# Turning an involution unit's sums with VectorE blocks and DRAM transfers instead of TensorE

## The chip, the cores and the metric

The kernel runs on one core of one Trainium2 chip. The metric is device time in microseconds for one execution, and the number compared is the median of several. Five engines work in parallel: TensorE (PE in the profile; its weight loads are PEld), VectorE (DVE), ScalarE (ACT), GpSimd (POOL) and SyncE (SP), which here issues nearly all transfers. Each has its own instruction stream; semaphores order them. SBUF and PSUM tiles have 128 partitions[...].

## The reference

Four images of 512 channels, 64 x 64 pixels, all float32. The first layer is self-attention over the 4096 pixels of an image, the second an involution: a 7 x 7 filter whose weights differ from pixel to pixel and are shared by 16 channels.

```python
# layer 0
q, k, v = wq@x + bq, wk@x + bk, wv@x + bv          # 128 channels each
attn = softmax(einsum('bci,bcj->bij', q, k))       # 4096 x 4096
x = wo @ einsum('bcj,bij->bci', v, attn) + bo + x
# layer 1
o1 = relu((W1 @ x) * s1 + b1)                      # 128 channels
w  = Ws @ relu((Wr @ o1) * sr + br) + bs           # 49 taps x 8 groups per pixel
inv[c, h, w_] = sum over 49 taps of w[group(c), tap, h, w_] * o1[c, h+dy, w_+dx]
x = (W3 @ inv) * s3 + b3 + x
```

## The kernel before, in words

An image is worked through in eight chunks of 512 pixels (eight rows). `keys_values` computes keys and values of all chunks at the start of an image. `attention` then takes one chunk of queries at a time: 32 steps, each with a score matmul (`pss`), an exponential on ACT (`pt`), a matmul with the values (`po`) and an addition on DVE of `pt` into the running denominators (`pacc`, L646). One step takes about 1.7 us on TensorE. There are five `pt` buffers, two PSUM buffers for scores and two PSUM buffers of the tag "mm", which all the small matmuls share.

Everything else is woven into these steps. After each step `chores` advances three generators by a step: `finishing` (denominators, output projection `pwo`, its addition to `x` on DVE, the first layer of the involution `o1`), `closing` (below), and `involution`. How far each may advance is decided while the program is written out, by a running estimate `pe` of TensorE's time and the estimates `free` of the other engines. A scheduling layer then settles the order of each engine's stream from its own expectations; the engines carry that order out as it stands.

The `involution` works in units of four image rows: 16 units per image, two to a chunk. The pixels of a unit lie on partitions, so a unit's sums `acc` have shape 128 pixels x (2 x 4 x 128). DVE multiplies shifted pixel rows by weights (`prod`, L341), POOL adds the product to `acc` (L365), and two last POOL additions fold the four partial rows together (L376). The pixel rows come through DRAM: `finish_block` turns `o1` in blocks of 32 x 32 on DVE (`o1t`, L559), writes them to the DRAM image `pix` (L569), and `pump` reads windows of `pix` into an SBUF ring of twelve rows (L247).

`turn_unit` is the part that is changed. The last layer W3 needs the channels on partitions, so the sums of a unit must be turned from pixels x channels to channels x pixels. Before, TensorE transposes two 128 x 128 tiles per unit into a "mm" PSUM buffer `pa` (L393), ACT copies them to `accT` (L404), and after the second unit of a chunk `close_chunk` is queued: four matmuls `py` with W3, one "mm" buffer each, four DVE additions `x<-py` into the chunk `x` (L419), each of which frees its buffer, and the transfer of the finished chunk to `out` (L428). The chunk's buffer, one of six, is then loaded with a later chunk (L173).

In the fourth image, units that end after attention is done add on TensorE and turn their sums there together; these are not touched, and neither are any units of the fourth image.

Of the kernel before, what the change touches and what calls it, by code (L numbers as in the profile page):

```python
# [8 lines left out]
F32 = mybir.dt.float32  # L9
# [4 lines left out]
B, C, H, W = 4, 512, 64, 64  # L14
N = H * W
P = 128
CT = C // P
CH = 512
# [33 lines left out]
NT = UR // 2  # L52
# [15 lines left out]
DVE_OP, POOL_OP = 0.7, 1.28  # L68
# [6 lines left out]
TB = 32  # L75
# [6 lines left out]
def fast_path(  # L82
# [20 lines left out]
    nc = tc.nc  # L103

    def pool(name, bufs, **kw):
        return ctx.enter_context(tc.tile_pool(name=name, bufs=bufs, **kw))
# [6 lines left out]
    work1 = pool("work1", 1)  # L113
    work2 = pool("work2", 2)
    prods = pool("prods", 4)
    scratch = pool("scratch", 1, space=bass.MemoryType.DRAM)
# [18 lines left out]
    ring = const.tile([P, RING, K, P], F32, name="ring")  # L135
    pix = [
        scratch.tile([H + 2 * PAD, WP, P], F32, tag=f"pix{i}", name=f"pix{i}") for i in range(2)
    ]

    x_r = x.rearrange("b (t p) n -> b p t n", p=P)  # L140
# [6 lines left out]
    finishing, closing, units = [], [], []  # L147
# [4 lines left out]
    reds, sums_c = {}, {}  # L152
# [5 lines left out]
    def until(us):  # L158
        while pe < us and not tail:
            yield "wait"  # L160

    def pe_us(us):
        nonlocal pe
        pe += us

    def takes(engine, us):
        free[engine] = max(free[engine], pe) + us
        return free[engine]
# [33 lines left out]
    def w_slice(off, t):  # L202
        return wt[:, off + t * P : off + (t + 1) * P]

    def v1(i):
        return vec[:, i : i + 1]

    def mm(o, lhsT, rhs, start=True, stop=True, shared=1):
        pe_us(rhs.free_size() * PE_COLUMN / shared)
        return nc.tensor.matmul(o, lhsT=lhsT, rhs=rhs, start=start, stop=stop)  # L210
# [80 lines left out]
    def involution():  # L291
        nonlocal low, due
        while True:
# [80 lines left out]
            if accp is None:  # L374
                for n in (2, 1):
                    nc.gpsimd.tensor_tensor(  # L376
                        acc[:, :, :n, :], acc[:, :, :n, :], acc[:, :, n : 2 * n, :], ALU.add
                    )
            closing.append(turn_unit(b, u, acc, accp, takes("pool", POOL_OP * 1.5)))


    def turn_unit(b, u, acc, accp, done):
        c, k = divmod(u, 2)
        yield from until(done + 2.0)
        for _ in range(7 if tail else 0):
            yield
        last = (b, c) == (B - 1, NCH - 1)
        if last or k == 0:
            sums_c[b, c] = work1.tile([P, CH], F32, tag="accT", name=f"accT_{b}_{c}")
        pa = ps.tile([P, NT, P], F32, tag="mm", name=f"pa_{b}_{u}")  # L390
        if accp is None:
            for t in range(NT):
                nc.tensor.transpose(pa[:, t, :], acc[:, t, 0, :], ident)  # L393
            pe_us(0.25)
        else:

            accs = work1.tile([P, CH // P, P], F32, tag="o1t", name=f"accs_{b}_{u}")
            nc.scalar.copy(accs, accp.rearrange("p t d c -> p (t d) c"))
            for t in range(NT):
                parts = [acc[:, t, d, :] for d in range(4)] + [accs[:, 2 * t + d, :] for d in range(2)]  # L400
                for i, part in enumerate(parts):
                    mm(pa[:, t, :], part, ident, i == 0, i == len(parts) - 1)
        n = NT * P
        nc.scalar.copy(sums_c[b, c][:, k * n : (k + 1) * n], pa.rearrange("p t c -> p (t c)"))  # L404
        yield
        if last:
            closing.append(close_chunk(b, c, k * n, n, sums_c.pop((b, c))))
        elif k:
            closing.append(close_chunk(b, c, 0, CH, sums_c.pop((b, c))))


    def close_chunk(b, c, off, n, acc):
        xt = xs[b, c][:, :, off : off + n]
        yield
        for t in range(CT):
            py = ps.tile([P, CH], F32, tag="mm", name=f"py_{b}_{c}_{off}_{t}")[:, :n]
            mm(py, w_slice(O_W3, t), acc[:, off : off + n])
            takes("dve", DVE_OP * n / CH)
            nc.vector.scalar_tensor_tensor(  # L419
                xt[:, t, :], py, v1(V_S3 + t), xt[:, t, :], ALU.mult, ALU.add  # L420
            )
            if n < CH:
                nc.sync.dma_start(out_r[b, :, t, c * CH + off : c * CH + off + n], xt[:, t, :])
            for _ in range(2):
                yield
        takes("dma", X_US)
        if n == CH:
            nc.sync.dma_start(out_r[b, :, :, c * CH + off : c * CH + off + n], xt)  # L428
# [553 lines left out]
def attention_then_involution(tc, x, wts, vecs, out):  # L982
    nc = tc.nc
    with tc.tile_pool(name="verdict", bufs=1) as vpool:
        verdict = vpool.tile([1, 1], mybir.dt.int32, name="verdict")
        fast_path(tc, x, wts, vecs, out, verdict)
        again = nc.values_load(verdict[0:1, 0:1], min_val=0, max_val=1)
        with tc.If(again > 0):
            general_path(tc, x, wts, vecs, out)
# [85 lines left out]
```

## Time and profile before

| | |
|---|---|
| median of 3 runs | 2623.66 us (2622.92 to 2625.16) |
| the profiled execution | 2624.13 us, of which the span of the trace is 2622.3 us |
| TensorE busy | 2599.3 us, 99% |
| DVE busy | 1865.5 us, 71% |
| POOL busy | 1821.0 us, 69% |
| ACT busy | 857.2 us, 33% |
| transfers, mean busy share of the 16 DMA engines | 36% |
| span less TensorE's busy time | 23.0 us |

Busy time counts an engine's own work and not its waiting. A wait of another engine only matters where TensorE ends up waiting for it. Line numbers are those of the kernel before.

### The profile page before, as it was taken

Reading aid. Unit: us, or ns where it says so; the run is one execution under the profiler, and the core shown is the slowest. Engines: PE = TensorE matmul, PEld = TensorE weight load, DVE = VectorE, ACT = ScalarE, POOL = GpSimd, SP = SyncE. Lnnn points to the kernel's source line nnn. Section 1 sums busy time; section 2 is a strip of 40 time slices with the busy share of each in tenths; the row PEclk is TensorE's granted clock in tenths of the full one; section 3 lists DMA queues with packets and bytes.
Section 4 is the critical chain, followed back from the end, with each engine's and each line's share of the span. In section 5 each row is a group of like instructions: output and inputs, shape, how many; then the busy total and the mean of one; then the engine's idle time right before and its main releaser. Section 6 shows DMA issues by size and latency. Waiting matters only on the chain.

```text
span 2622.3 us, 24098 instructions
## 1 busy us (share of the span) xinstructions
PE 2599.3 (99%) x7382; PEld 1242.0 (47%) x7382; DVE 1865.5 (71%) x2626; ACT 857.2 (33%) x1430; POOL 1821.0 (69%) x1197
## 2 busy tenths in 40 slices
PE   9999999999999999999999999999999999999998
PEld 7444444445544444444554444444464444444574
DVE  0347887877575787888576677878757768787887
ACT  1333333332233333333223333333313333333330
POOL 0007887878781787888875467888787667777876
PEclk9999999999999999999999999999999999999999
DMA  6032323336514244322541433434453423222343
GB/s 235 0 74 60 75 64 75 69 89 156 139 40 106 60 93 92 87 71 61 153 116 36 103 61 92 93 92 93 92 154 88 107 60 89 68 61 60 77 91 101
DMA packets 143898, 231.70 MB, mean 88 GB/s; under 512 B 57032, under 2 KB 63632, under 8 KB 143632
## 3 DMA queue, kind: packets, MB, share of 16 engines
q1 hardware_dynamic: 143328, 229.71, 36.2%
q8 instruction: 60, 0.98, 0.2%
q14 instruction: 78, 0.64, 0.1%
q10 hardware_dynamic: 432, 0.36, 0.0%
HBM read 187.28 MB, written 42.77 MB: 88 GB/s over the span
## 4 chain that ended last, share of the span: by engine, by line
PE 94%; POOL 3%; DVE 2%; DMA 0%; issue 0%; ACT 0%; POOLq 0%; DVEq 0%; ACTq 0%
PE pss L210 34%; PE po L210 33%; PE pq L210 4%; PE pwo L210 4%; PE p L210 4%; PE py L210 4%; PE pv L210 4%; PE pk L210 3%; POOL acc L365 3%; PE pw L210 2%; DVE prod L341 1%; PE pr L210 1%; PE pa L393 0%; PE accp L210 0%; DVE x L419 0%
## 5 line engine op out<-in xcount | busy, mean ns | idle before, releaser
L365 POOL TENSOR_TENSOR acc<-acc,prod 128x768 f32<-128x768 f32 (+3 forms) x1063 | 1699.0, 1616 | 777.0 <-DVE prod L341 726.2
L210 PE MATMUL pss<-q,k 128*128 128x512 f32 (+1 forms) x2112 | 1055.0, 584 | 2.3 <-ACT q L471 2.3
L210 PE MATMUL po<-pt,v 128*128 128x512 f32 (+1 forms) x2112 | 1047.5, 580 | 0.0
L615 ACT ACTIVATE pt<-pss 128x512 f32<-128x512 f32 x1024 | 611.5, 597 | 1225.6 <-PE pss L210 1201.7
L341 DVE TENSOR_TENSOR prod<-ring,pw 128x512 f32<-128x512 f32 (+3 forms) x1092 | 902.1, 850 | 100.7 <-POOL acc L365 87.7
L646 DVE TENSOR_TENSOR pacc<-pacc,pt 128x512 f32<-128x512 f32 x958 | 666.2, 695 | 379.7 <-ACT pt L615 372.9
L210 PEld LDWEIGHTS po<-pt,v 128*128 128x128 f32 x2112 | 399.3, 190 | 480.3 <-issue 460.2
L210 PEld LDWEIGHTS pss<-q,k 128*128 128x128 f32 x2112 | 389.6, 190 | 452.3 <-issue 432.6
L210 PE MATMUL py<-accT,wt 128*128 128x512 f32 (+1 forms) x264 | 132.8, 586 | 7.8 <-DVE x L419 6.7
L210 PE MATMUL pwo<-on,wt 128*128 128x512 f32 (+1 forms) x264 | 129.3, 583 | 0.0
L210 PEld LDWEIGHTS pv<-wt,x 128*128 128x128 f32 x1024 | 121.7, 195 | 15.8 <-issue 15.6
L515 DVE SCALAR_TENSOR_TENSOR x<-pwo,bo,x 128x512 f32<-128x512 f32 (+1 forms) x132 | 96.3, 734 | 45.5 <-PE pwo L210 44.0
L376 POOL TENSOR_TENSOR acc<-acc 128x512 f32<-128x512 f32 x120 | 119.5, 996 | 9.4
L210 PE MATMUL pv<-wt,x 128*128 128x128 f32 x1024 | 123.3, 279 | 0.0
L341 DVE TENSOR_TENSOR acc<-ring,pw 128x1024 f32<-128x1024 f32 (+1 forms) x84 | 79.4, 964 | 61.1 <-PE pw L210 58.9
L533 ACT ACTIVATE x<-x,vec 128x512 f32<-128x512 f32 (+1 forms) x132 | 92.8, 706 | 81.5 <-PE p L210 76.4
L210 PE MATMUL p<-x,wt 128*128 128x512 f32 (+1 forms) x264 | 119.2, 579 | 0.0
L210 PE MATMUL pk<-x,wt 128*128 128x512 f32 x256 | 117.1, 597 | 0.3 <-DMA x<-x_dram 0.3
L419 DVE SCALAR_TENSOR_TENSOR x<-py,vec,x 128x512 f32<-128x512 f32 (+1 forms) x132 | 95.9, 726 | 29.8 <-PE py L210 28.1
L210 PE MATMUL pq<-x,wt 128*128 128x512 f32 (+1 forms) x264 | 115.5, 580 | 0.0
L210 PEld LDWEIGHTS py<-accT,wt 128*128 128x128 f32 x264 | 49.3, 191 | 65.3 <-issue 48.5
L210 PEld LDWEIGHTS pq<-x,wt 128*128 128x128 f32 x264 | 49.8, 190 | 58.7 <-issue 56.4
(58 smaller groups left out, 723.0 us busy)
## 6 DMA issues: line engine op xcount, KB each, us to landing
x<-x_dram SPq DMA_DIRECT2D x55, 1024.0 KB, 6.0
ring<-pix SPq DMA_DIRECT2D x74, 448.0 KB, 10.9
ring<-pix SPq DMA_DIRECT2D x24, 1344.0 KB, 18.3
out_dram<-x SPq DMA_DIRECT2D x31, 1024.0 KB, 4.4
ring<-pix SPq DMA_DIRECT2D x24, 896.0 KB, 14.0
ring<-pix SPq DMA_DIRECT2D x30, 672.0 KB, 11.2
ring<-pix SPq DMA_DIRECT2D x6, 2240.0 KB, 19.1
pix<-o1t SPq DMA_DIRECT2D x192, 32.0 KB, 1.7
```

The costliest lines, as they stand in the source:

```text
L210: return nc.tensor.matmul(o, lhsT=lhsT, rhs=rhs, start=start, stop=stop)
L341: nc.vector.tensor_tensor(prod[:, :, p0 : p0 + n, :].rearrange("p t d (g c) -> p t d g c", g=G), image.rearrange("p t d (g c) -> p t d g c ...
L365: nc.gpsimd.tensor_tensor(acc[:, :, d0 : d0 + n, :], acc[:, :, d0 : d0 + n, :], prod[:, :, :n, :], ALU.add,)
L376: nc.gpsimd.tensor_tensor(acc[:, :, :n, :], acc[:, :, :n, :], acc[:, :, n : 2 * n, :], ALU.add)
L419: nc.vector.scalar_tensor_tensor(xt[:, t, :], py, v1(V_S3 + t), xt[:, t, :], ALU.mult, ALU.add)
L515: nc.vector.scalar_tensor_tensor(xt[:, t, :], pw, bo[:, t : t + 1], xt[:, t, :], ALU.add, ALU.add)
L533: nc.scalar.activation(xt[:, t, :], xt[:, t, :], AF.Identity, bias=v1(V_B3 + t))
L615: nc.scalar.activation(pt, pss, AF.Exp)
L646: nc.vector.tensor_tensor(paccs[k], paccs[k], pt, ALU.add)
```

## The change

In `turn_unit`, for every unit of the first three images, the two TensorE transposes and the ACT copy are replaced. DVE turns the sums in blocks of 32 x 32 within each strip of 32 partitions into a tile `turned` (two buffers). SP writes its four strips of 32 partitions to a DRAM scratch tile `turns` (two buffers, alternating by chunk), placed so that the blocks land at their final channels and pixels. After the second unit of a chunk SP reads the chunk's `turns` back as `accT` with channels on partitions. Pauses of three steps of the closing queue stand between the turn and the writes, between the writes and the read, and between the read and `close_chunk`. The tile `accT` is now made when it is read back and not at the first unit.

```diff
+    turns = [
+        scratch.tile([CH // P, P, P], F32, tag=f"turns{i}", name=f"turns{i}") for i in range(2)
+    ]
...
         yield from until(done + 2.0)
         for _ in range(7 if tail else 0):
             yield
+        if accp is None and b < B - 1:
+            blocks = work2.tile([P, NT * P], F32, tag="turned", name=f"turned_{b}_{u}")
+            takes("dve", DVE_OP * NT * P / CH)
+            nc.vector.transpose(
+                blocks.rearrange("p (t k q) -> p t k q", t=NT, q=TB),
+                acc[:, :, 0, :].rearrange("p t (k q) -> p t k q", q=TB),
+            )
+            for _ in range(3):
+                yield
+            turn = turns[c % 2]
+            for i in range(P // TB):
+                rows = slice(i * TB, (i + 1) * TB)
+                nc.sync.dma_start(
+                    turn[k * NT : (k + 1) * NT, :, rows]
+                    .rearrange("t (k a) q -> a (t k) q", a=TB),
+                    blocks[rows].rearrange("p (k q) -> p k q", q=TB),
+                )
+            if k:
+                for _ in range(3):
+                    yield
+                sums_c[b, c] = work1.tile([P, CH], F32, tag="accT", name=f"accT_{b}_{c}")
+                nc.sync.dma_start(
+                    sums_c[b, c].rearrange("p (t x) -> p t x", x=P),
+                    turn.rearrange("t c x -> c t x"),
+                )
+                for _ in range(3):
+                    yield
+                closing.append(close_chunk(b, c, 0, CH, sums_c.pop((b, c))))
+            return
         last = (b, c) == (B - 1, NCH - 1)
```

## The prediction

> **What bounds the kernel now.** I read the chain of waits first. It lies on TensorE almost throughout:
>
> ```profile
> PE 94%; POOL 3%; DVE 2%; DMA 0%; issue 0%; ACT 0%; POOLq 0%; DVEq 0%; ACTq 0%
> ```
>
> So each microsecond of matmul taken away is a microsecond won, as long as nothing makes TensorE wait. Next, the transposes by their tile and one of them in TensorE's timeline:
>
> ```profile
> L393 PE MATMUL pa<-ident,acc x120: 272/273/329, 240.6 to 2536.7; 128*128 128x128 f32 x120
> ...
> 320.54 1.02 PE L210 MATMUL po<-pt,v 128*128 128x512 f32 x2
> 321.39 0.38 PE L393 MATMUL pa<-ident,acc 128*128 128x128 f32 x2
> 321.61 1.02 PE L210 MATMUL pss<-q,k 128*128 128x512 f32 x2
> ```
>
> The 273 ns are a pipelined duration. What a pair costs is seen from start to start: 321.61 - 321.39 = 0.22 us. Last, TensorE's waits: it hardly waits, and what it does wait for is DVE freeing a PSUM buffer of `py`, the three times where an image begins:
>
> ```profile
> PE py L210 <- DVE x L419: 6.7, 3, 2.4
> ```
>
> **What the skill says.** The Trainium skill, "PSUM — Partial Sum Buffer", section "Engine vs sequencer instructions": the queues of ScalarE, VectorE and GpSimd are strict FIFO. An operation that waits holds all behind it. The trace of before agrees: at 1327.06 us a `prod` waits 2.67 us for the ring and everything behind stands. "VectorE: DVE Perf Modes", "The three transpose paths": VectorE turns 32 x 32 blocks only, so the crossing between strips is left to the transfers; the trace shows the same pair for `o1t`. "DMA: Bandwidth & Descriptors", "Anatomy of one DMA — SWDGE (gpsimd) path": about 2.0 us fixed per DMA. The kernel's like transfers, issued by SP, land in 1.7 us.
>
> **The change part by part.**
>
> *Removed.* 48 units x one pair x 0.22 us = **10.4 us** of TensorE, all on its path. 48 ACT copies of 0.37 us go too and win nothing: ACT is busy 33%.
>
> *Added on DVE.* 48 block turns of 128 x 256. The nearest row is the turn of 128 x 512 at L559, 707 ns; half is 0.36 us (bounds 0.3 and 0.7). 17 us in all on an engine 71% busy, beside TensorE: nothing by itself.
>
> *Added on SP.* 192 writes of 32 KB, like this row, and 24 reads of 256 KB, which I put at 2.5 to 4.1 us from the 128 KB and 256 KB rows:
>
> ```profile
> pix<-o1t SPq DMA_DIRECT2D x192, 32.0 KB, 1.7
> ```
>
> After the last turn of a chunk that is some 4 x 0.5 + 1.7 + 4 = 8 us. In the built program's order `py` stands 30 us and more behind the second turn (neighbouring steps at 344 and 379 us for chunk 1), with SP quiet in between. I cost the detour itself at nothing; its cover is those steps. Chunk by chunk `py` moves about 20 us back (chunk 1: 360 to 379 us), so the chunk's output and the next load go back too. Chunk 6 has its buffer at about 330 us instead of 311 and is used at 460: nothing. The odd case is the start of an image, below.
>
> *Moved: what DVE now waits for.* This is the part that decides. Before, the transposes waited for POOL's final sum inside TensorE's stream, in most units 6 to 9 us after it was there. In the built program the turn stands in DVE's stream much earlier, among steps that ran before POOL was done. For each of the 48 units I compared the end of the DVE operation just ahead of the turn with the end of POOL's last addition, both in the trace of before: POOL is later every time, by 2.2 to 8.8 us, 5.6 on average. So DVE will stand still some 270 us in all. It has the room, and the `pacc` behind the turn do too: `pt` has five buffers, and TensorE would only miss a `pacc` that is about 9 us late. What has no such room is `x<-py`, which frees one of two "mm" buffers. Unit 4 of image 0, in the built order:
>
> ```
> DVE:  turned_0_4, pacc, x<-py_0_1_0_0, pacc, pacc, x<-py_0_1_0_1
> PE:   py_0_1_0_0, pss, po, pss, po, pr, py_0_1_0_1, pw, pw, ...
> ```
>
> `py_1` takes the buffer of `py_0` (`pr` has the other). POOL's and TensorE's timelines around it:
>
> ```profile
> 375.06 7.69 POOL L365 TENSOR_TENSOR acc<-acc,prod 128x512 f32<-128x512 f32 x8
> 382.83 2.08 POOL L376 TENSOR_TENSOR acc<-acc 128x512 f32<-128x512 f32 x2
> ...
> 382.43 1.02 PE L210 MATMUL po<-pt,v 128*128 128x512 f32 x2
> 383.38 0.65 PE L210 MATMUL pr<-o,wt 128*64 128x256 f32 x4
> 383.96 0.93 PE L210 MATMUL pw<-wt,red 33*128 33x392 f32 x4
> ```
>
> The sums are there at 384.91. Then DVE: turn 0.36, `pacc` 0.70, `x<-py` 0.73; the buffer is free at 386.7. TensorE came to this place at 383.96, and now has three `py` (0.86 us each) and a transpose pair less behind it: 383.96 - 2.58 - 0.22 = 381.2. POOL does not come earlier, it ran without a gap from 354.7 us on. **Idle: 5.5 us.** Unit 10 has the same order with one more `pacc`: POOL ends at 601.22, free at 603.7; TensorE arrives at 600.30 + 0.86 (`pw` is now ahead) - 2.80 = 598.4: 5.3 us. In unit 2 `x<-py` follows the turn at once: 312.3 + 0.36 + 0.73 = 313.4 against 311.7: 1.7 us. Per image 12.5 us; the same places recur in images 1 and 2 with the same distances.
>
> *The start of an image.* `turned_12` stands ahead of `o1t_7` on DVE, and its writes ahead of the writes of `o1t_7` on SP. Image 1:
>
> ```profile
> 1300.77 0.70 DVE L559 STREAM_TRANSPOSE o1t<-o 128x512 f32<-128x512 f32 x1
> ...
> 1327.06 0.42 DVE L341 TENSOR_TENSOR prod<-ring,pw 128x256 f32<-128x256 f32 x1 [2.67 <-DMA ring<-pix]
> ```
>
> POOL ends unit 12 at 1309.6, so `o1t_7`, and behind it `pix` and the ring, go back by about 9 us, for a `prod` that already waits on the ring. A 1 MB output that went ahead of the ring is now behind it and gives back 2 to 4 us. Seven late products later comes the new image's first `pacc`, which has some 5 us of room: 1 to 4 us of TensorE idle, I take 2.5. The 2.2 us that TensorE lost there on `py` before (6.7 in 3) should go, since those `py` stand later: 0.3 net per image.
>
> *Sum.* 3 x (12.5 + 0.3) - 10.4 = +28 us on the profiled execution's 2624.1, and the median of the runs lies 0.5 us under that: **2652 us**, 1.1% slower. A measurement of this kernel can tell about 0.2% (5 us) from no change.
>
> **Rivals.**
>
> *TensorE does not wait and the 10.4 us are won.* For it: transfers have 30 us of cover, DVE has idle time, POOL is in no hurry. The mechanism is POOL's lead: at units 2, 4 and 10 it would have to end 2 to 6 us earlier against TensorE than in the trace of before, and from 1.2 us of idle per place (10.4 / 9) on, the change loses. Against it: POOL ran unit 4 without a gap. Time 2613, or 2607 if the waits at the image starts go too.
>
> *The waits only cancel.* If TensorE's lead of 2.8 us is used up otherwise, the idle is 2.7, 2.5 and 0 per image, 15.6 in all, and without the image starts the result is +5: 2629.
>
> *Worse: the units fall behind.* The wait at a turn puts the next unit back by up to 4 us. POOL took 32.7 us for unit 4, from its first product at 352.2, and a unit has 36. If the delay is carried on, every unit's turn catches `pacc` and `x<-pwo` as well, and each of 24 chunks loses 2 us more: 2700.
>
> *Transfers late.* If reads land 20 us late behind ring loads (18 us for the largest), some `py` wait for DMA. Cover of 30 us speaks against it; 3 image starts x 5 us would be +15 on the forecast, 2667.
>
> *It does not do what it says:* the built order shows the pairs gone and the turns there; excluded.
>
> **How the numbers follow.** Won without waits 0.15; cancel 0.13; waits at the nine places 0.52, 2635 to 2672 by itself; transfers late 0.10; falling behind 0.10. The range runs from 2612, the win, to 2685, which leaves out most of falling behind. Slower by over 0.2%: 0.74; within 0.2%: 0.08, the middle of cancelling; faster: 0.18.
>
> **What would show it.** TensorE's busy time down by about 10 us and its idle up by about 40; a wait "PE py <- DVE x" of some 35 us in nine or more times, the longest near 5; DVE waiting some 270 us for POOL at the turn; no wait of `py` for `accT`. Right about the work and wrong about the wait if "PE py <- DVE x" stays under 10 us; wrong about the transfers if `py` waits for DMA.

## The result, and the profile after

The changed kernel takes **2661.1 us** (median of 4 runs, 2659.99 to 2663.23) against 2624.41 us of the kernel before on the same chip: ratio 1.0141, 95% interval 1.0128 to 1.0153. It is slower by 36.7 us; the prediction said 28 us, 2652, and its range held the time. The profiled execution took 2659.99 us, of which the span is 2658.2 us, so the spans differ by 35.9 us. One execution in the experiments, of the kernel with transfers only, ran in a slower state of the chip (2728.14 us, granted clock 0.948) and is left out of its ratio. Line numbers from here on are those of the changed kernel, or of the experiment named.

The chain of waits is no longer nearly all TensorE. POOL, DVE, transfers and a share with nothing to wait for ("issue") have grown in it:

```profile
PE 81%; POOL 8%; issue 4%; DVE 4%; DMA 2%; SPq 1%; ACT 0%; POOLq 0%; DVEq 0%; ACTq 0%
```

The list of TensorE's waits (what waits, for what; us in total, times, longest) answers the single line of before, 6.7 us in three waits:

```profile
PE py L215 <- DVE x L454: 18.6, 10, 2.8
PE pss L215 <- ACT pt L650: 13.0, 4, 4.3
PE p L215 <- DVE x L550: 3.1, 1, 3.1
```

The first line is the predicted wait, at half the predicted size. The second is the late start of the images, predicted smaller; the third was not foreseen. DVE's list shows where the lateness starts, and that it is not DVE's work: the turn itself is one short row of the page, with its idle time in the last column.

```profile
DVE turned L396 <- POOL acc L381: 238.2, 48, 8.7
DVE pacc L681 <- ACT pt L650: 237.3, 216, 4.9
...
DVE prod L346 <- DMA ring<-pix: 44.4, 10, 8.6
```

```profile
L396 DVE STREAM_TRANSPOSE turned<-acc 128x256 f32<-128x256 f32 x48 | 21.4, 446 | 238.2 <-POOL acc L381 238.2
```

The transfers of the detour, in the list of DMA issues (KB each, median us to landing), are as quick as the like ones of before:

```profile
turns<-turned SPq DMA_DIRECT2D x192, 32.0 KB, 1.7
accT<-turns SPq DMA_DIRECT2D x24, 256.0 KB, 2.8
```

Unit 4 of image 0 again, the place that the prediction worked through: POOL, DVE and TensorE in the timeline of the changed kernel.

```profile
381.47 2.06 POOL L381 TENSOR_TENSOR acc<-acc 128x512 f32<-128x512 f32 x2
...
383.57 0.45 DVE L396 STREAM_TRANSPOSE turned<-acc 128x256 f32<-128x256 f32 x1 [4.42 <-POOL acc L381]
383.94 0.67 DVE L681 TENSOR_TENSOR pacc<-pacc,pt 128x512 f32<-128x512 f32 x1
384.51 0.73 DVE L454 SCALAR_TENSOR_TENSOR x<-py,vec,x 128x512 f32<-128x512 f32 x1
...
380.06 1.02 PE L215 MATMUL pss<-q,k 128*128 128x512 f32 x2
...
381.87 0.65 PE L215 MATMUL pr<-o,wt 128*64 128x256 f32 x4
385.30 1.12 PE L215 MATMUL py<-accT,wt 128*128 128x512 f32 x2 [2.77 <-DVE x L454]
386.35 1.54 PE L215 MATMUL pw<-wt,red 33*128 33x392 f32 x4
387.82 2.07 PE L215 MATMUL pss<-q,k 128*128 128x512 f32 x2
389.69 1.92 PE L215 MATMUL po<-pt,v 128*128 128x512 f32 x2
```

Read down the middle: the turn waits for POOL, then `pacc`, then `x<-py`, which ends at 385.24, and TensorE's next `py` starts at 385.30. That is the predicted chain, step for step. What was not predicted stands in the last two lines: a pair of score matmuls takes 2.07 us there, and 1.02 us at 380.06. The windows view gives the granted clock of such stretches (start:end, length, TensorE's busy time and instructions, clock, DMA share, GB/s):

```profile
375.00:395.00 20.00, 17.23 (x38) 0.83 0.53 101
...
300.00:320.00 20.00, 17.65 (x46) 1.00 0.40 76
1350.00:1370.00 20.00, 16.13 (x32) 0.83 0.62 141
```

In the trace's clock records TensorE's clock drops to 0.500 for 3.4 or 6.8 us around many of its pauses. This costs time that no wait shows, and lengthens TensorE's *busy* time.

I therefore split each span in three: the gaps between TensorE's matmuls, half of the time at clock 0.500 outside these gaps, and the rest.

| kernel (span, us) | gaps | lost at half clock | rest |
|---|---|---|---|
| before (2622.3) | 16.2 | 5.1 | 2601.0 |
| changed (2658.2) | 43.8 | 19.5 | 2594.9 |
| turn held in place (2604.5) | 9.7 | 1.7 | 2593.1 |
| turn only (2646.0) | 31.8 | 10.4 | 2603.8 |
| transfers only (2623.5) | 15.9 | 6.8 | 2600.8 |
| removal only (2610.3) | 14.0 | 5.1 | 2591.2 |
| held in unit 12 (2643.5) | 30.6 | 18.1 | 2594.8 |
| held in units 2, 4, 10 (2628.1) | 24.1 | 9.9 | 2594.1 |
| `py` later (2618.0) | 16.0 | 8.5 | 2593.5 |

The last column is steady: 2601 to 2604 where TensorE's transposes are there, 2591 to 2595 where they are gone. So the 35.9 us are + 27.6 of gaps, + 14.4 of half clock and - 6.1 of the rest. The removal alone should have brought some 10 in that column; about 4 us are not accounted for.

### The profile page after: what moved, and what is told of

It reads as the page before. It is cut to its first block, busy times and chain, and to the rows that moved or that the text cites. A ratio compares the mean times of both kernels' runs of the same rounds, so it can differ in the third digit from the quotient of the medians.

```text
span 2658.2 us, 24165 instructions
## 1 busy us (share of the span) xinstructions
PE 2607.4 (98%) x7286; PEld 1232.9 (46%) x7286; DVE 1870.4 (70%) x2674; ACT 838.0 (32%) x1382; POOL 1822.4 (69%) x1197
## 4 chain that ended last, share of the span: by engine, by line
PE 81%; POOL 8%; issue 4%; DVE 4%; DMA 2%; SPq 1%; ACT 0%; POOLq 0%; DVEq 0%; ACTq 0%
PE pss L215 28%; PE po L215 28%; POOL acc L370 7%; PE pq L215 4%; PE pv L215 4%; PE py L215 3%; PE pwo L215 3%; PE pk L215 3%; PE p L215 3%; PE pw L215 2%; DVE prod L346 2%; DMA ring<-pix 2%; POOL acc L381 1%; DVE pacc L681 1%; DVE x L454 1%
## 5 line engine op out<-in xcount | busy, mean ns | idle before, releaser
L396 DVE STREAM_TRANSPOSE turned<-acc 128x256 f32<-128x256 f32 x48 | 21.4, 446 | 238.2 <-POOL acc L381 238.2
L215 PE MATMUL py<-accT,wt 128*128 128x512 f32 (+1 forms) x264 | 134.9, 594 | 19.4 <-DVE x L454 18.6
## 6 DMA issues: line engine op xcount, KB each, us to landing
ring<-pix SPq DMA_DIRECT2D x6, 2240.0 KB, 19.5
```

What stands on the lines that cost most here:

```text
L396: nc.vector.transpose(blocks.rearrange("p (t k q) -> p t k q", t=NT, q=TB), acc[:, :, 0, :].rearrange("p t (k q) -> p t k q", q=TB),)
```

## The experiments

My theory (W): the removal wins about 10 us; the turn stands in DVE's stream ahead of the time at which POOL is done, DVE waits there, and whatever stands close behind the turn and is needed by TensorE comes late. The rivals: the transfers cost the time, through the queue or through late data; or DVE's standing time as such does.

### The turn held in its place in the source

`keep_in_program_order` tells the scheduling layer to leave an instruction behind what the source puts ahead of it.

```diff
-            nc.vector.transpose(
+            tc.keep_in_program_order(nc.vector.transpose(
                 blocks.rearrange("p (t k q) -> p t k q", t=NT, q=TB),
                 acc[:, :, 0, :].rearrange("p t (k q) -> p t k q", q=TB),
-            )
+            ))
```

> The changed kernel with one thing different: the DVE turn keeps its place in the order in which the program is written, behind the DVE operations written before it, 5 to 14 us later in DVE's stream than in the changed kernel and after POOL's last sum. Transfers, steps and removed transposes are those of the changed kernel. Theory W (the loss comes from DVE standing at the turn and waiting for POOL, with x<-py and the late products behind it): the wait of DVE at the turn falls from 238 us to under 15 us, the waits of TensorE for x<-py and for pt at the image starts go, and so do the stretches of half clock that follow them; time 2606 to 2617 us, faster than before. Theory T (the detour through DRAM costs it: 216 more transfers on SP's queue and their small packets): the transfers are all still there, so 2650 us or more.

Measured: 2607.49 us (2606.3 to 2607.93, 5 runs), ratio to before 0.9937, interval 0.9924 to 0.9951. The wait at the turn is gone from DVE's list, and no wait in TensorE's list, apart from the program's start and the last image, is longer than 0.8 us:

```profile
PE pss L215 <- ACT q L506: 2.3, 3, 0.8
...
PE pq L215 <- DVE x L454: 0.8, 1, 0.8
```

The same turns and the same transfers, with another place for the turn, make a kernel that is 54 us faster than the changed one and faster than the kernel before. So neither the turn's work nor the detour is the price; the place is.

### One part at a time: turn, transfers, removal

The first puts the turn into the kernel before and uses its result for nothing; the transposes stay.

```diff
+        if accp is None and b < B - 1:
+            blocks = work2.tile([P, NT * P], F32, tag="turned", name=f"turned_{b}_{u}")
+            takes("dve", DVE_OP * NT * P / CH)
+            nc.vector.transpose(
+                blocks.rearrange("p (t k q) -> p t k q", t=NT, q=TB),
+                acc[:, :, 0, :].rearrange("p t (k q) -> p t k q", q=TB),
+            )
```

> The kernel before, with TensorE's transposes and ACT's copies kept, and one DVE turn of each unit's sums added, whose result nothing reads; no transfers. In the built order the turn stands as early as in the changed kernel, but x<-py, which has not been moved, stands ahead of it in units 2, 4 and 10. It tells the wait at the turn from what stands behind it. Theory W: DVE waits 200 to 270 us for POOL, TensorE's waits for x<-py stay near 7 us, and only the image starts lose (o1t of the last chunk behind the turn of unit 12, then the ring, then the first pacc): 3 x (4 to 8) us, so 2634 to 2648 us. Theory T: no transfer was added, so 2624 plus or minus 4 us.

Measured: 2649.22 us (2647.83 to 2652.07, 4 runs), ratio 1.0100, interval 1.0084 to 1.0115. DVE's and TensorE's waits, in this order:

```profile
DVE turned L390 <- POOL acc L376: 234.2, 48, 8.7
```

```profile
PE py L210 <- DVE x L426: 16.8, 3, 5.7
PE p L210 <- DVE x L522: 2.6, 1, 2.6
```

DVE stands as long as in the changed kernel, but TensorE pays mainly at three places, the image starts, with 5.5 to 5.7 us each, where it lost 2.1 to 2.4 us before. The expectation missed here: these waits are for `x<-py`, and the first `pacc` of an image costs nothing; the time lies 1 us above its range. At units 2, 4 and 10 nothing happens: with the transposes in place, `py` runs where it ran before, away from the next turn. So those waits need two parts of the change together, the early turn and the detour that puts `py` some 20 us back, close behind a turn.

The second adds the 192 writes and 24 reads to the kernel before, from a weight tile and into a tile that nobody uses.

```diff
+            turn = turns[c % 2]
+            for i in range(P // TB):
+                rows = slice(i * TB, (i + 1) * TB)
+                nc.sync.dma_start(
+                    turn[k * NT : (k + 1) * NT, :, rows]
+                    .rearrange("t (k a) q -> a (t k) q", a=TB),
+                    wt[rows, : NT * P].rearrange("p (k q) -> p k q", q=TB),
+                )
+            if k:
+                spare = work1.tile([P, CH], F32, tag="spare", name=f"spare_{b}_{c}")
+                nc.sync.dma_start(
+                    spare.rearrange("p (t x) -> p t x", x=P), turn.rearrange("t c x -> c t x")
+                )
```

> The kernel before, complete, and beside it the 192 writes and 24 reads of the changed kernel, with the same shapes and the same scratch tiles, taking their data from a weight tile that is ready from the start, into a tile that nothing reads; no DVE turn. Theory W: transfers are covered, 2624 plus or minus 5 us. Theory T: 216 issues and 13 MB in 128-byte and 512-byte pieces delay the ring and the loads, 2640 to 2665 us.

Measured: 2624.96 us (2622.83 to 2625.59, 12 runs), ratio 1.0002, interval 0.9993 to 1.0010. TensorE's list begins with the line of before:

```profile
PE py L213 <- DVE x L436: 6.7, 3, 2.4
```

The transfers cost nothing that can be measured.

The third takes the transposes and copies out of the first three images and puts nothing in their place; `py` multiplies a weight tile instead of the sums.

```diff
+        if accp is None and b < B - 1:
+            yield
+            if k:
+                closing.append(close_chunk(b, c, 0, CH, wt[:, :CH]))
+            return
```

> The kernel before, leaving out the transposes of the sums and the copies in the first three images; py multiplies a weight tile instead of the sums, so the involution's share of the output of these images is left out. It measures the term of 10.4 us by itself. Expected 2624 - 10.4 = 2613 to 2614 us if 0.22 us per pair is right, down to 2607 us if the waits for x<-py at the image starts go with it. If the pairs were hidden by something, 2620 us or more.

Measured: 2612.16 us (2610.31 to 2613.34, 5 runs), ratio 0.9954, interval 0.9941 to 0.9968: 11.5 us won (8 to 15 by the interval), 0.24 us for a pair if all of it is theirs. In the table the last column falls by 9.8 us, 0.20 us for a pair, and the gaps by 2.2. The old `py` waits at the image starts stay, 6.9 us in three.

### Where the turn hurts

Two runs hold the turn in place for some units only.

```diff
+            if u == 12:
+                tc.keep_in_program_order(turned)
```

> The changed kernel with the turn held at the place of the source text (behind what the source puts ahead of it in VectorE's stream) for unit 12 alone, the last unit of an image. It isolates the start of the next image. Theory W (each turn that stands early makes VectorE wait for POOL, and what is queued behind that turn comes late to TensorE: here the sums that free turned_12's followers up to the first pacc): TensorE's waits of its pss on ACT's pt at the image starts (4 of them, 13.0 us, in the changed kernel) go, with the part of TensorE's slow clock that follows those pauses (some 5 us); its py waits for x (10, 18.6 us) stay. About 2643 us, 2639 to 2647, against 2661.1. Rival R (the image start is late because the transfers of the turned sums, 48 writes and 24 reads, stand in front of the pixel ring's loads in the queues): the pss waits stay at about 13 us and the time at 2658 to 2663.

Measured: 2645.41 us (2643.37 to 2649.01, 5 runs), ratio 1.0081, interval 1.0067 to 1.0094. TensorE's list:

```profile
PE py L215 <- DVE x L456: 18.0, 9, 2.8
PE p L215 <- DVE x L552: 2.8, 1, 2.8
...
PE pss L215 <- ACT pt L652: 0.8, 3, 0.3
```

The `pss` waits are gone but for 0.8 us and the `py` waits stay, as W said. By itself this does not rule out the rival, because the writes of unit 12 have moved together with its turn: they are issued from 688.98 us on, behind the first loads of the ring, where the changed kernel had them ahead. The traces together do. At the first image start the ring's loads begin at 674.00 us before, at 684.81 with the turn only and no transfer of turned sums, and at 686.47 in the changed kernel. So of the 12.5 us by which the ring is later the turn alone brings 10.8, which leaves 1.7 for the transfers in front of it and all else. This one turn per image is worth some 16 us (1.0141 - 1.0081 = 0.60% of 2625; the two intervals leave about 5 us either way). I had put 18: the half clock fell by only 1.4 us and not by 5.

```diff
+            if u in (2, 4, 10):
+                tc.keep_in_program_order(turned)
```

> The changed kernel with the turn held at the place of the source text for units 2, 4 and 10 alone. Theory W: TensorE's py waits for x (10, 18.6 us) go, with the part of the slow clock that follows them (some 12 us of the 14); the pss waits at the image starts (4, 13.0 us) stay. About 2631 us, 2626 to 2637. Rival Q (any turn that stands early costs in like measure, since VectorE's lateness only moves to the next unit): the py waits reappear at units 3, 5 and 11 or at others, sum 12 us or more, and the time is 2648 or above.

Measured: 2630.38 us (2629.85 to 2632.6, 11 runs), ratio 1.0023, interval 1.0014 to 1.0032. TensorE's list begins:

```profile
PE pss L215 <- ACT pt L652: 11.8, 3, 4.2
PE p L215 <- DVE x L552: 3.1, 1, 3.1
```

No `py` wait for `x` is left, and none has moved to other units. Three turns per image are worth 31 us, of which the gaps are 43.8 - 24.1 = 19.7 and the half clock 9.6. The two runs together make up 47 of the 54 us; what remains holds, among others, the `p` wait of 3.1 us, which both keep.

### The turn left early, `py` moved away from it

A longer pause in the closing queue keeps every turn early, but puts 17 to 27 DVE operations between the turns of units 2, 4 and 10 and the next `x<-py`, where the changed kernel has none to two.

```diff
-                for _ in range(3):
+                for _ in range(8):
                     yield
                 closing.append(close_chunk(b, c, 0, CH, sums_c.pop((b, c))))
```

> The changed kernel with the sums of a unit's last chunk closed later in the source (8 steps of the stream in place of 3 between the attention product and its closing), which leaves every turn early in VectorE's stream but puts 20 or more VectorE operations between a turn and the next copy x<-py behind it. Theory W: VectorE still waits some 240 us at the turn, but the copy is no longer late: the py waits of units 2, 4 and 10 (18.6 us) go; the pss waits at the image starts (13 us) stay or grow, since x comes later there. 2628 to 2640. Rival V (the sheer time that VectorE stands at the turn, 238 us, costs TensorE, wherever the copy is): the time stays within 5 us of 2661 with other waits of the same sum.

Measured: 2617.68 us (2615.26 to 2620.2, 8 runs), ratio 0.9971, interval 0.9961 to 0.9982. DVE's list first, the first line of TensorE's second:

```profile
DVE turned L396 <- POOL acc L381: 228.0, 48, 8.7
DVE pacc L681 <- ACT pt L650: 222.0, 201, 4.9
```

```profile
PE pk L215 <- DMA x<-x_dram: 6.7, 3, 2.3
```

DVE stands 228 us at the turn, nearly as long as in the changed kernel, and the kernel is faster than before. So nearly all of the standing time costs nothing, and rival V falls: `pacc`, behind the turn, waits less for `pt` in turn. Before, that wait was

```profile
DVE pacc L646 <- ACT pt L615: 372.9, 342, 4.9
```

and here it is 222.0 us. What the standing time may still cost is at most the 9 us (0.9971 - 0.9937 of 2624) by which this run is slower than the turn held in its place.

My expectation was wrong in one half, and the time lies 10 us below its range. I had the `pss` waits at the image starts stay; they went too, and TensorE waits there for `x` to be loaded, 2.2 to 2.3 us before each. SP's timeline at the first of them shows what holds up the load:

```profile
666.32 1.81 SPq L405 DMA_DIRECT2D turns<-turned  x4
...
670.19 0.40 SPq L178 DMA_DIRECT2D x<-x_dram  x1
```

It stands in SP's queue behind the writes of unit 12's turn and four writes of `o1t`, and that turn ended only at 666.29, after 8.75 us of waiting for POOL. Issued at 670.19, the load lands 5.9 us later, and `pk` starts at 676.20. The order is the same at the other two image starts. So these 6.7 us, too, hang on the late turn, by way of the transfer queue. That the pause at `pk` gives the ring the time that `pss` lacked is possible, but no run separates it.

Of all versions, the turn held in its place is the fastest: 2607.5 us, with the detour through DRAM kept.

## Why the prediction came out as it did

*Removal.* 10.4 us predicted, 11.5 measured on its own, with 8 to 15 as its interval. Right.

*The turn and the transfers.* A turn took 0.446 us, not 0.36, still inside the bounds given. Writes landed in 1.7 us and reads in 2.8, as put; costing these transfers at nothing is confirmed by the run with transfers alone. That the detour also moves `py` back is not free: it is one half of the waits at units 2, 4 and 10.

*DVE at the turn.* 238 us in 48 waits, 8.7 the longest, for a predicted 270 and 8.8. The method, comparing DVE's place in the built order with POOL's end in the trace of before, holds. It agrees with what was taken from the skill's page "PSUM — Partial Sum Buffer", section "Engine vs sequencer instructions", on strict FIFO queues: in unit 4 the `x<-py`, whose matmuls had ended at 378.5, stood behind the turn until 384.51.

*Units 2, 4 and 10: right places, wrong sizes.* Predicted per image 1.7, 5.5 and 5.3; measured in image 0: 2.35, 2.77 and 0.84. In sum 18.6 us for a predicted 37.5. This is the term that failed, mostly by its form: I worked out each place against the trace of before, as if the others did not exist. But a pause makes TensorE later at the next place, and so shortens the wait there. Unit 10 shows it best: TensorE was 7.0 us later than I had it (605.4 for 598.4), while DVE freed the buffer only 2.5 us later (606.2 for 603.7). By then ten pairs of transposes were gone, not the one that I took off, which gives 596.4; two pauses of 2.35 and 2.77 us and half of 6.8 us at half clock add 8.5 and make 604.9. Carried forward, 5.3 becomes 0.84. In unit 4 this is half of the miss: TensorE came to `py` at 382.5, not at 381.2, after losing 2.35 us in unit 2. The other half is POOL, which I had said would not come earlier: its run of additions began at 353.32, not at 354.67, and it ended at 383.53, not at 384.91. Unit 2 has no pause ahead of it. There TensorE came 1.8 us earlier than I had it (309.95 for 311.7) and the buffer 1.1 us earlier (312.3 for 313.4), so that wait grew. All this is worked out from the traces; no run holds the turn of one of these units alone.

*The image start: right chain, too small.* The new image's first `pacc` was to be late by 1 to 4 us. DVE's and TensorE's timelines at the first of them:

```profile
675.50 0.45 DVE L396 STREAM_TRANSPOSE turned<-acc 128x256 f32<-128x256 f32 x1 [8.75 <-POOL acc L381]
675.87 0.67 DVE L594 STREAM_TRANSPOSE o1t<-o 128x512 f32<-128x512 f32 x1
...
702.45 2.28 DVE L346 TENSOR_TENSOR prod<-ring,pw 128x256 f32<-128x256 f32 x5 [7.71 <-DMA ring<-pix]
...
711.28 0.69 DVE L679 COPY pacc<-pt 128x512 f32<-128x512 f32 x1
...
712.71 1.12 PE L215 MATMUL pss<-q,k 128*128 128x512 f32 x2 [3.86 <-ACT pt L650]
```

The turn of unit 12 keeps `o1t` 8.75 us; the ring arrives late, DVE stands 7.71 us for it, then does the late products, and comes to `pacc` at 711.28. Until then ACT has no free `pt`, so that it empties no score buffer, and TensorE waits for one. It lost 3.9 to 4.3 us at each of the three, and 1.0 once more: 13.0 us for a predicted 7.5. The old 6.7 us of `py` waits went, as predicted. Holding that one turn in place removed all but 0.8 us of it.

*Not foreseen.* The 14.4 us of half clock, the largest miss. The `p` wait of 3.1 us at 2088, behind the turn of unit 15 in image 2: I had looked for `x<-py` behind turns, and here it was `x<-pwo`, which makes the `x` that `p` reads. And the 4 us that are open.

From + 28: - 18.9 (units), + 5.5 (image starts), + 3.1 (`p`), + 14.4 (clock), + 4 (open) gives 36. So the total of 28 was near by luck: an over-sized term and a missing one nearly cancelled. Of the signs that I named, "busy time down by about 10" was wrong for this reason: it rose from 2599.3 to 2607.4 us, because matmuls at half clock last longer; idle rose by 28, not by 40; `py` waited 18.6 us in ten waits, not 35; `py` waited for `accT` no more than the 0.5 us of the last image.

Of the rivals, "the 10 us are won" is what the turn held in place does, with 2607 as worked out; it needed another order, and not a faster POOL. "The units fall behind" did not occur: POOL's last addition in unit 10 ended 2.4 us later than before and TensorE was later there by more than that. "The waits only cancel" and "transfers late" did not occur either: TensorE waited 18.6 us for `x<-py`, and no `py` waited for a transfer.

## What to carry to other kernels

When an operation moves from one engine's queue to another's, look first at what stands behind it in the new queue and who waits for that; here 48 turns of 0.45 us, in the wrong place, cost 54 us, and one line of code that fixed the place won it back. A long wait in a queue may cost little, as 228 us did in one run, if nothing urgent stands within its length behind it, in that queue or in the transfer queue that waits with it. When several waits are worked out from one trace, carry each one's delay forward to the next, or their sum is too large; and price a pause of TensorE above its length (here 14.4 us of half clock came with 27.6 us of gaps).

## What the runs showed of the hardware

TensorE's clock falls around short pauses. In the nine traces there are 41 stretches at clock 0.500 while TensorE still had work: 28 of 3.4 us and 13 of 6.8 us. Each begins within a pause of TensorE of at least 1.88 us or up to 2.1 us after its end; 38 of the 46 pauses of 2 us and more had one, and only 3 of the 51 between 0.7 and 2 us. Pauses of one length may have one or not: in the changed kernel one of 2.35 us at 957.6 had 6.8 us at half clock, one of the same length at 309.9 had none.

The Trainium skill, "TensorE: Matmul & The Clock Gate", section "Part 1: The HAM clock gate (the "warmup" mystery)", describes a gate that halves the clock after an idle window of about 3.4 us, with windows that run freely. The stretches of one or two times 3.4 us and the chance in them agree with this. The size of the pause does not: 2.1 to 2.4 us were often enough here, and 3.86 us once were not. That the pauses bring the drops rests on their standing together in nine traces; no run tried it by itself.
